# The sum over four attention heads: five VectorE products and additions, or one product and four TensorE matmuls with an identity

## The chip, the core and the metric

The kernel runs on one NeuronCore of a Trainium2 chip, in float32 throughout. The metric is the device time of one execution in microseconds, as the median of the runs made. A profiled execution, with the hardware profiler recording every instruction, is a separate execution with its own time.

## The reference, cut to what matters

The model is two graph layers over 12,500 nodes with 256 features and 200,000 edges sorted by destination. The first is a pair of GCN convolutions; the second is an attention layer with four heads of 64 channels. The change touches only the end of the second:

```python
xt = jnp.matmul(x, weight).reshape(-1, heads, out_ch)          # (n, 4, 64)
alpha_l = jnp.einsum('ehd,hd->eh', xt[row], attn_l)
alpha_r = jnp.einsum('ehd,hd->eh', xt[col], attn_r)
alpha = jax.nn.softmax(jax.nn.leaky_relu(alpha_l + alpha_r, 0.01), axis=1)
tmp = jnp.einsum('nh,nhd->nd', alpha[:n], xt[col[:n]])         # sum over 4 heads
out = jnp.broadcast_to(tmp[:, None, :], (n, heads, out_ch))
...
x = x + out
```

Only the first n = 12,500 edges matter for the output. For each of them four weights (a softmax over the heads) multiply four vectors of 64 channels of that edge's destination node; the four products are added, and the sum of 64 channels is added to each of the four quarters of the node's row.

## The kernel before, in words

`fast_path` runs in four stages. A preparation stage sorts out the chunks of edges and normalises x. Two edge stages (`convolve`, called twice) then walk over 1,563 tiles of 128 edges each: GpSimd (POOL) gathers 128 rows of a table for each tile with an indirect DMA (L1086, tile `fgot`), and TensorE (PE) multiplies them by a 0/1 matrix that adds edges to their destinations (L1091, `facc`). Each has a pool of four buffers of 14 gathered tiles, so a gather waits when PE has not yet read the buffer that it is to fill.

The last stage, the pool named `fmixes`, is the attention, and it is where the change lies. It covers 98 tiles of 128 nodes in 15 groups: 13 groups of seven tiles, one of four, one of three. Two functions do the work of a group g:

- `ends_of(g)`: for each tile of the group one matmul (`fends`, L1345, 260 columns) picks the destination rows, and ScalarE (ACT) copies the result from PSUM into the group's SBUF tile `fxg` (L1347). The `fends` PSUM tile has two buffers, so a matmul waits for the copy two before it. For groups 0 and 1 this was done earlier, in the second edge stage (tiles `fxe`). Every second group, VectorE (DVE) also makes a 0/1 matrix for later groups (`hot_t`, L1258).
- `mix(g)`: POOL gathers the group's logits (`fal`, L1355, seven indirect DMAs of 128 rows of four numbers). DVE adds the other half of the logits (L1359), for groups 0 and 1 also a correction `lacks` that PE makes with 21 small matmuls (L1326, L1361), applies the leaky ReLU, takes the maximum and subtracts it (L1362 to L1365). ACT takes the exponential (L1366). DVE sums, inverts and scales (L1367 to L1371) into the PSUM tile `share`, 4 weights for each of 128x7 nodes. Then come the lines that the change replaces: two products of two heads each, `near` into SBUF and `far` into PSUM (L1378), and three additions, `some`, `more` and `fmix` (L1381, L1383, L1385). Last, `fres` (L1387) adds the sum to the four quarters of the residual rows `fxr`, and SyncE (SP) stores the group.

The order of the work is the order of the program text, written out by hand; no scheduler moves it, and each engine runs its own instructions in order. The closing loop is

```python
for g in range(len(groups) + 2):
    if g < len(groups):
        keep(g)
        ends_of(g)
    if g >= 2:
        mix(g - 2)
```

so that every engine's list alternates: `ends_of(g)`, then `mix(g - 2)`, then `ends_of(g + 1)`, then `mix(g - 1)`. On ACT, therefore, the seven copies of group g stand before the exponential of group g - 2. On PE, before the change, the tail holds nothing but `fends` and, for the first two groups, `lacks`.

Of the kernel before, what the change touches and what calls it, by code (L numbers as in the profile page):

```python
# [8 lines left out]
F32 = mybir.dt.float32  # L9
# [8 lines left out]
P = 128  # L18
# [395 lines left out]
def fast_path(  # L414
# [26 lines left out]
    nc = tc.nc  # L441
    N, D = x.shape
    (E,) = src.shape
    H, C = attn_l.shape
# [13 lines left out]
    G = 7  # L458
# [23 lines left out]
    ident = const.tile([P, P], F32, name="fident")  # L482
# [27 lines left out]
    with tc.tile_pool(name="fprep", bufs=1) as prep:  # L510
# [86 lines left out]
        for k in range(NPT):  # L597
            p = perm[:, k, :Q[k], :]
# [23 lines left out]
        near = prep.tile([NCH, CE], F32, name="near_f")  # L622
# [51 lines left out]
        with tc.tile_pool(name="wpsum", bufs=2, space=PSUM) as psum:  # L674
# [7 lines left out]
            for i in range(KC):  # L682
                pw = psum.tile([P, D], F32, name="fw")
                for k in range(KC):
                    nc.tensor.matmul(pw, wpt[:, k, i * P:(i + 1) * P], wa[:, k, :],
                                     start=(k == 0), stop=(k == KC - 1))
                nc.scalar.activation(wf[:, i, :], pw, AF.Copy)
            pw = psum.tile([P, D], F32, name="fw")
            for k in range(KC):
                nc.tensor.matmul(pw[:1, :], bp[:, k:k + 1], wa[:, k, :], start=(k == 0),  # L690
                                 stop=(k == KC - 1))
# [158 lines left out]
        psum = wpsum.enter_context(tc.tile_pool(name="kpsum", bufs=1, space=PSUM))  # L850
# [4 lines left out]
        some = prep.tile([P, 1], F32, name="degs")  # L855
# [395 lines left out]
    def load_ends(pool, c, bufs):  # L1251
        to_all = pool.tile([P, CE], I32, name="to_all", bufs=bufs)
        nc.sync.dma_start(to_all, dst[c * CE:(c + 1) * CE].partition_broadcast(P))
        return to_all

    def turn_hots(pool, c, to_all, bufs):
        hot_t[c] = pool.tile([P, CE], F32, name="hot_t", bufs=bufs)
        nc.vector.tensor_scalar(hot_t[c], to_all, base_b[:, c:c + 1], lane,  # L1258
                                op0=ALU.subtract, op1=ALU.is_equal)
# [38 lines left out]
    with tc.tile_pool(name="fmixes", bufs=2) as mp, \  # L1298
            tc.tile_pool(name="apsum", bufs=1, space=PSUM) as psum:
        late = {c: load_ends(mp, c, 3) for c in range(EARLY, EARLY + 3)}  # L1300

        def turn_late(c):
            if c in late:
                turn_hots(mp, c, late[c], 3)
                if c + 3 < AC:
                    late[c + 3] = load_ends(mp, c + 3, 3)

        ends, kept = {}, {}


        groups = [(t, G) for t in range(0, NT - G, G)] + [(NT - G, 4), (NT - 3, 3)]
        assert G == 7 and J % G == 0

        def keep(g):
            t0, n = groups[g]
            kept[g] = mp.tile([P, G, D], F32, name="fxr", bufs=3)
            nc.sync.dma_start(kept[g][:, :n, :], kept_x[t0 * P:(t0 + n) * P, :].rearrange(
                "(c p) d -> p c d", p=P))

        def missing(g):  # L1320

            px = psum.tile([P, G, H], F32, name="lacks", bufs=1)
            for i in range(G):
                t = groups[g][0] + i
                for k in range(LW):
                    nc.tensor.matmul(px[:, i, :], hot_l[k][:, t * P:(t + 1) * P],  # L1326
                                     lates[NT - LW + k][:, DR:], start=(k == 0),
                                     stop=(k == LW - 1))
            return px

        def ends_of(g):

            t0, n = groups[g]
            if t0 < J:
                ends[g] = early[g]
                if g + 1 == J // G:
                    turn_late(1)
                return
            xa = ends[g] = mp.tile([P, G, DR], F32, name="fxg", bufs=4)
            for i in range(n):  # L1340
                c, j = divmod(t0 + i, J)
                if j == 0:
                    turn_late(c + 1)
                px = psum.tile([P, DR], F32, name="fends", bufs=2)
                nc.tensor.matmul(px, hot_t[c][:, j * P:(j + 1) * P], rows[c], start=True,  # L1345
                                 stop=True)
                nc.scalar.activation(xa[:, i, :], px, AF.Copy)  # L1347

        def mix(g):
            (t0, n), xa, xr = groups[g], ends.pop(g)[:, :groups[g][1], :], kept.pop(g)  # L1350
            xr = xr[:, :n, :]
            al = mp.tile([P, G, H], F32, name="fal", bufs=4)
            for i in range(n):
                c, j = divmod(t0 + i, J)
                nc.gpsimd.indirect_dma_start(  # L1355
                    out=al[:, i, :], out_offset=None, in_=(table_l if c else table_e)[:],
                    in_offset=bass.IndirectOffsetOnAxis(ap=src_t[:, c, j:j + 1], axis=0))
            s = mp.tile([P, G, H], F32, name="fs")[:, :n, :]
            nc.vector.tensor_add(s, al[:, :n, :], xa[:, :, D:])  # L1359
            if t0 < J:  # L1360
                nc.vector.tensor_add(s, s, missing(g))  # L1361
            nc.vector.scalar_tensor_tensor(s, s, SLOPE, s, op0=ALU.mult, op1=ALU.max)  # L1362
            m = mp.tile([P, G], F32, name="fm")[:, :n]
            nc.vector.tensor_reduce(m, s, AX.X, ALU.max)
            nc.vector.tensor_sub(s, s, m[:, :, None].to_broadcast([P, n, H]))  # L1365
            nc.scalar.activation(s, s, AF.Exp)  # L1366
            nc.vector.tensor_reduce(m, s, AX.X, ALU.add)  # L1367
            nc.vector.reciprocal(m, m)

            share = psum.tile([P, G, H], F32, name="share", bufs=1)[:, :n, :]  # L1370
            nc.vector.tensor_mul(share, s, m[:, :, None].to_broadcast([P, n, H]))  # L1371
            xh = xa[:, :, :D].rearrange("p g (h c) -> p g h c", h=H)
            h2 = H // 2
            near = mp.tile([P, h2, G, C], F32, name="near")[:, :, :n, :]
            far = psum.tile([P, h2, 512], F32, name="far", bufs=1)
            far = far[:, :, :n * C].rearrange("p h (g c) -> p h g c", c=C)
            for v, o in ((near, 0), (far, h2)):
                nc.vector.tensor_mul(v.rearrange("p h g c -> p g h c"), xh[:, :, o:o + h2, :],  # L1378
                                     share[:, :, o:o + h2, None].to_broadcast([P, n, h2, C]))
            some = mp.tile([P, G, C], F32, name="some")[:, :n, :]  # L1380
            nc.vector.tensor_add(some, near[:, 0], far[:, 0])  # L1381
            more = psum.tile([P, G, C], F32, name="more", bufs=1)[:, :n, :]
            nc.vector.tensor_add(more, near[:, 1], far[:, 1])  # L1383
            mixed = psum.tile([P, G, C], F32, name="fmix", bufs=1)[:, :n, :]
            nc.vector.tensor_add(mixed, some, more)  # L1385
            res = mp.tile([P, G, D], F32, name="fres", bufs=2)[:, :n, :]
            nc.vector.tensor_add(res.rearrange("p g (h c) -> p g h c", h=H),  # L1387
                                 xr.rearrange("p g (h c) -> p g h c", h=H),
                                 mixed[:, :, None, :].to_broadcast([P, n, H, C]))
            n0, n1 = t0 * P, min((t0 + n) * P, N)  # L1390
            k, r = divmod(n1 - n0, P)
            if k:
                nc.sync.dma_start(out[n0:n0 + k * P, :].rearrange("(c p) d -> p c d", p=P),
                                  res[:, :k, :])
            if r:
                nc.sync.dma_start(out[n0 + k * P:n1, :], res[:r, k, :])

        assert H == 4
# [6 lines that stand above are left out]
# [41 lines left out]
```

## Time and profile before

| what | value |
|---|---|
| median of 3 runs | 4234.17 us (4231.9 to 4235.17) |
| profiled execution | 4963.54 us, its span 4961.4 us |
| mean granted TensorE clock in it | 0.710 |
| busy share of the span | POOL 62%, PE 54%, DVE 24%, ACT 8% |
| attention stage in it | from the first `fends` at 4752.25 us to the end of the span, 209.2 us |
| busy in 4750 to 4962 us | DVE 108.0 us, POOL 94.1, PE 89.0, ACT 36.4 |
| `near`, `far` of a group of seven | 1.09 us each, 896 elements a partition |
| `some`, `more`, `fmix` of such a group | 0.62 to 0.63 us each, 448 elements a partition |
| `fres` of such a group | 2.02 us, 1792 elements a partition |
| `fends` | 84 matmuls in this stage, each two records of 260 columns, 587 ns mean |

A row of the table of groups reads: line, engine, operation, output<-input, shape, count, then busy microseconds and the mean nanoseconds of one, then the idle time just before and what ended it. The timeline has the start, the duration in microseconds, engine, line, operation and tiles, and in brackets the idle time before it. A float32 matmul shows as two records. Ends of PE records are modelled, not measured; the wait of the engine that needs a PE result is measured.

### The profile page before, as it was taken

The page shows a single profiled execution, that of the slowest core. Times are in us where ns is not written, and L with a number is a line of the kernel's source. Part 1 is how long each engine was busy: PE and PEld are TensorE (multiplying, and loading weights), DVE is VectorE, ACT ScalarE, POOL GpSimd, SP SyncE. Part 2 cuts the span into 40 slices and gives each one's busy share as a digit, 9 for nine tenths or more (in the row PEclk, how much of TensorE's full clock was granted, in tenths as well). Part 3 has the DMA queues.
Part 4 walks back from the last instruction along what each step waited for, and adds up shares of the span by engine and source line. Part 5 has one row for each costly group of instructions (what it writes and reads, how often), then busy time and mean ns, then how long its engine had stood idle before and what let it go on. Part 6 is the DMA issues. An engine that isn't in the chain of part 4 may idle for free. (4 is left out here: it accounts for less than half of the span.)

```text
span 4961.4 us, 31747 instructions
## 1 busy us (share of the span) xinstructions
PE 2702.2 (54%) x10363; PEld 2052.2 (41%) x10363; DVE 1215.4 (24%) x2571; ACT 408.9 (8%) x1067; POOL 3088.9 (62%) x3304
## 2 busy tenths in 40 slices
PE   5356565555555665555444555555464545555553
PEld 4244443333334444333334444444454445444441
DVE  7122111111111111111222222222122222222236
ACT  5000000000000000000000100010011001001011
POOL 1666666666666666666566666666666666666633
PEclk7667676666676676667677777777777777777766
DMA  7433333333333333333334433443343434444435
GB/s 225 115 102 105 105 107 105 105 107 104 103 103 105 106 107 104 104 105 105 111 97 113 116 105 106 110 110 107 101 111 105 111 108 109 111 114 109 108 102 158
DMA packets 325910, 551.10 MB, mean 111 GB/s; under 512 B 96009, under 2 KB 224232, under 8 KB 325736
## 3 DMA queue, kind: packets, MB, share of 16 engines
q0 software_dynamic: 153520, 414.27, 31.0%
q1 hardware_dynamic: 126678, 118.54, 7.9%
q10 hardware_dynamic: 45538, 16.17, 1.3%
q8 instruction: 86, 1.41, 0.1%
q14 instruction: 88, 0.72, 0.1%
HBM read 495.47 MB, written 53.19 MB: 111 GB/s over the span
## 5 line engine op out<-in xcount | busy, mean ns | idle before, releaser
L1086 POOL DMA_INDIRECT fgot<-ftable,fsrc_t x3126 | 2965.6, 949 | 1621.6 <-issue 911.1
L1091 PE MATMUL facc<-fgot,fhot 128*128 128x257 f32 (+1 forms) x6252 | 1876.5, 441 | 629.3 <-issue 594.5
L1091 PEld LDWEIGHTS facc<-fgot,fhot 128*128 128x128 f32 x6252 | 1350.4, 224 | 999.1 <-issue 774.1
L1037 DVE TENSOR_TENSOR buf<-buf,fturn 128x256 f32 x224 | 94.4, 422 | 2092.0 <-remote 1725.3
L1014 DVE TENSOR_TENSOR fhot<-iota_p,to_t 128x1792 f32<-128x1792 f32 x224 | 448.4, 2003 | 0.1
L1200 PE MATMUL fpt<-fident,h 128*128 128x128 f32 x194 | 59.6, 405 | 586.2 <-ACT h L1195 462.1
L1120 PE MATMUL fpo<-wf,buf 128*128 128x256 f32 x388 | 145.3, 513 | 309.7 <-DVE buf L1037 217.1
L1200 PEld LDWEIGHTS fpt<-fident,h 128*128 128x128 f32 x194 | 26.8, 187 | 625.7 <-ACT h L1195 486.3
L1120 PEld LDWEIGHTS fpo<-wf,buf 128*128 128x128 f32 x388 | 96.4, 258 | 358.5 <-issue 250.7
L1174 PE MATMUL fpo<-fwo,fz 128*128 128x256 f32 x388 | 124.8, 451 | 214.6 <-issue 122.7
L1165 DVE SCALAR_TENSOR_TENSOR fy<-rb,fb2c,fpz 128x128 f32<-128x128 f32 x194 | 58.7, 344 | 722.8 <-remote 390.5
L1021 ACT ACTIVATE fsums<-facc 128x257 f32<-128x257 f32 (+1 forms) x224 | 85.9, 383 | 1740.8 <-remote 1229.7
L1179 DVE SCALAR_TENSOR_TENSOR fx<-fpo,fdinv,fxb 128x256 f32<-128x256 f32 x97 | 46.9, 483 | 714.0 <-remote 453.9
L1174 PEld LDWEIGHTS fpo<-fwo,fz 128*128 128x128 f32 x388 | 76.8, 217 | 228.6 <-issue 125.5
L1158 PE MATMUL fpz<-buf,fwb 128*128 128x128 f32 x776 | 158.2, 372 | 12.0 <-DVE buf L1037 12.0
L977 PE MATMUL fturn<-fident,fsums 128*128 128x128 f32 x448 | 107.5, 330 | 93.8 <-ACT fsums L1021 56.8
L1213 PE MATMUL fpx<-fwg,ht 128*128 128x4 f32 (+1 forms) x388 | 62.8, 270 | 175.6 <-ACT ht L1204 119.0
L1158 PEld LDWEIGHTS fpz<-buf,fwb 128*128 128x128 f32 x776 | 150.1, 285 | 14.9 <-DVE buf L1037 13.9
L1213 PEld LDWEIGHTS fpx<-fwg,ht 128*128 128x128 f32 x388 | 64.1, 210 | 190.2 <-ACT ht L1204 125.9
L977 PEld LDWEIGHTS fturn<-fident,fsums 128*128 128x128 f32 x448 | 75.5, 175 | 146.6 <-ACT fsums L1021 67.9
L1355 POOL DMA_INDIRECT fal<-table_l,fsrc_t x84 | 80.4, 957 | 73.7 <-DVE fs L1362 49.0
L1345 PE MATMUL fends<-rows,hot_t 128*128 128x260 f32 x168 | 72.8, 587 | 92.1 <-issue 57.2
(213 smaller groups left out, 1633.8 us busy)
## 6 DMA issues: line engine op xcount, KB each, us to landing
fgot<-ftable,fsrc_t POOLq DMA_INDIRECT x3126
ftable<-fxt SPq DMA_DIRECT2D x14, 910.0 KB
self<-ftable SPq DMA_DIRECT2D x97, 130.0 KB
ftable<-fo ACTq DMA_DIRECT2D x98, 128.0 KB
kept_x<-fx SPq DMA_DIRECT2D x98, 128.0 KB
self<-ftable SPq DMA_DIRECT2D x97, 128.0 KB
fxb<-in_x_dram SPq DMA_DIRECT2D x97, 128.0 KB
fxt<-in_x_dram SPq DMA_DIRECT2D x13, 896.0 KB
```

The costliest lines, as they stand in the source:

```text
L977: nc.tensor.transpose(v["pt"][:, i * KC + k, :], rows[:, k * P:(k + 1) * P], ident)
L1014: nc.vector.tensor_tensor(h[:, :n, :], iota_p[:, None, :].to_broadcast([P, n, P]), to_t[:, c, :n, None].to_broadcast([P, n, P]), ALU.is_equal)
L1021: nc.scalar.activation(sb, acc, AF.Copy)
L1037: nc.vector.tensor_add(b, b, v["pt"][:, :KC, :])
L1086: nc.gpsimd.indirect_dma_start(out=got, out_offset=None, in_=table[:], in_offset=bass.IndirectOffsetOnAxis(ap=src_t[:, c, j:j + 1], axis=0))
L1091: nc.tensor.matmul(acc, hots[c][:, j, :], got[:, :width], start=(j == 0), stop=(j == nj[c] - 1))
L1120: nc.tensor.matmul(po, buf[:, k, :P], wf[:, k, :], start=(k == 0), stop=False)
L1158: nc.tensor.matmul(pz[:, m, :], wb[:, k, m * P:(m + 1) * P], buf[:, k, :P], start=(k == 0), stop=(k == KC - 1))
L1174: nc.tensor.matmul(po, v["z"][:, m, :], wo[:, m, :], start=(m == 0), stop=(m == KC - 1))
L1200: nc.tensor.transpose(pt[:, k, :], v["h"][:, k * P:(k + 1) * P], ident)
L1213: nc.tensor.matmul(px, v["ht"][:, k, :], wg[:, k, d0:], start=(k == 0), stop=(k == KC - 1))
L1355: nc.gpsimd.indirect_dma_start(out=al[:, i, :], out_offset=None, in_=(table_l if c else table_e)[:], in_offset=bass.IndirectOffsetOnAxis(a ...
```

## The change

The two products and three additions become one product over all four heads, written head by head into one SBUF tile `part`, and four matmuls that accumulate into one PSUM tile, each with the identity `fident` as one operand and one head's 64 channels of all the group's tiles (448 columns) as the other. `fmix` gets two PSUM buffers in place of one; the PSUM tiles `far` and `more` go.

```diff
             share = psum.tile([P, G, H], F32, name="share", bufs=1)[:, :n, :]
             nc.vector.tensor_mul(share, s, m[:, :, None].to_broadcast([P, n, H]))
-            xh = xa[:, :, :D].rearrange("p g (h c) -> p g h c", h=H)
-            h2 = H // 2
-            near = mp.tile([P, h2, G, C], F32, name="near")[:, :, :n, :]
-            far = psum.tile([P, h2, 512], F32, name="far", bufs=1)
-            far = far[:, :, :n * C].rearrange("p h (g c) -> p h g c", c=C)
-            for v, o in ((near, 0), (far, h2)):
-                nc.vector.tensor_mul(v.rearrange("p h g c -> p g h c"), xh[:, :, o:o + h2, :],
-                                     share[:, :, o:o + h2, None].to_broadcast([P, n, h2, C]))
-            some = mp.tile([P, G, C], F32, name="some")[:, :n, :]
-            nc.vector.tensor_add(some, near[:, 0], far[:, 0])
-            more = psum.tile([P, G, C], F32, name="more", bufs=1)[:, :n, :]
-            nc.vector.tensor_add(more, near[:, 1], far[:, 1])
-            mixed = psum.tile([P, G, C], F32, name="fmix", bufs=1)[:, :n, :]
-            nc.vector.tensor_add(mixed, some, more)
+
+            part = mp.tile([P, H, G, C], F32, name="part")[:, :, :n, :]
+            nc.vector.tensor_mul(part.rearrange("p h g c -> p g h c"),
+                                 xa[:, :, :D].rearrange("p g (h c) -> p g h c", h=H),
+                                 share[:, :, :, None].to_broadcast([P, n, H, C]))
+            mixed = psum.tile([P, G, C], F32, name="fmix", bufs=2)[:, :n, :]
+            for h in range(H):
+                nc.tensor.matmul(mixed, ident, part[:, h], start=(h == 0), stop=(h == H - 1))
             res = mp.tile([P, G, D], F32, name="fres", bufs=2)[:, :n, :]
```

On PE the four matmuls of `mix(g - 2)` now stand after the `fends` (and `lacks`) of its iteration and before the `fends` of group g + 1; on DVE `fres` follows the product directly.

## The prediction

> **What bounds the kernel now.** I read the page first, for where the time lies, then POOL's waits, then the timeline and windows of the attention stage, which alone the change touches. The gathers of the two edge stages fill most of the span:
>
> ```profile
> L1086 POOL DMA_INDIRECT fgot<-ftable,fsrc_t x3126 | 2965.6, 949 | 1621.6 <-issue 911.1
> ```
>
> A gather is 949 ns and the step to the next some 0.29 us. Of the 1621.6 us that POOL idles before gathers, 911.1 is that step; most of the rest is in these two rows of its waits:
>
> ```profile
> POOL fgot L1086 <- remote: 465.1, 116, 11.4
> POOL fgot L1086 <- PE facc L1091: 158.7, 18, 10.8
> ```
>
> With three small rows behind PE (20.6, 5.3 and 4.2) that is 654 us in which POOL waits for a buffer that PE should long have read. The profiled execution took 4963.5 us, of which 2.1 lies around the span, the runs 4234.2: 729 less. The two numbers are nearly the same once the attention stage is added, where PE shows the same sickness:
>
> ```profile
> 4857.51 0.39 ACT L1347 ACTIVATE fxg<-fends 128x260 f32<-128x260 f32 x1 [5.22 <-remote]
> 4857.95 1.24 PE L1345 MATMUL fends<-rows,hot_t 128*128 128x260 f32 x2 [4.38 <-ACT fxg L1347]
> ...
> 4862.40 0.39 ACT L1347 ACTIVATE fxg<-fends 128x260 f32<-128x260 f32 x1 [4.50 <-remote]
> ```
>
> ACT's copy needs nothing but the matmul, yet waits 4.5 to 5.2 us for one that is modelled at 1.24. There are three such spells: DVE waits 18.7 us for `lacks` until 4785.90, the next five `fends` take some 20 us instead of 5, DVE's sum after the exponential waits 14.9 us at 4869.96 and 10.95 at 4914.01. That is 18.7 + 15 + 14.9 + 11 = 60 us; 654 + 60 = 714 of the 729. I conclude that the spells belong to the profiled execution and that the timed attention stage is about 209 - 70 = 140 us. So I read its pace between the spells:
>
> ```profile
> 4837.47 0.18 DVE L1359 TENSOR_TENSOR fs<-fal,fxg 128x28 f32<-128x28 f32 x1
> ...
> 4838.40 0.23 ACT L1366 ACTIVATE fs<-fs 128x28 f32<-128x28 f32 x1 [2.12 <-issue]
> ...
> 4838.96 5.33 PE L1345 MATMUL fends<-rows,hot_t 128*128 128x260 f32 x14 [1.73 <-issue]
> 4839.12 0.20 DVE L1371 TENSOR_TENSOR share<-fs,fm 128x28 f32<-128x28 f32 x1
> 4839.35 1.09 DVE L1378 TENSOR_TENSOR near<-fxg,share 128x896 f32<-128x896 f32 x1
> 4840.35 1.09 DVE L1378 TENSOR_TENSOR far<-fxg,share 128x896 f32<-128x896 f32 x1
> 4841.47 0.62 DVE L1381 TENSOR_TENSOR some<-near,far 128x448 f32<-128x448 f32 x1
> 4842.01 0.62 DVE L1383 TENSOR_TENSOR more<-near,far 128x448 f32<-128x448 f32 x1
> 4842.67 0.63 DVE L1385 TENSOR_TENSOR fmix<-some,more 128x448 f32<-128x448 f32 x1
> 4843.33 2.02 DVE L1387 TENSOR_TENSOR fres<-fxr,fmix 128x1792 f32<-128x1792 f32 x1
> 4845.27 1.21 DVE L1258 TENSOR_SCALAR hot_t<-to_all,base_b,lane 128x1792 f32<-128x1792 int32 x1
> 4846.39 0.18 DVE L1359 TENSOR_TENSOR fs<-fal,fxg 128x28 f32<-128x28 f32 x1
> ```
>
> DVE is never idle here but for the exponential: a group is 8.92 us with `hot_t` (4837.47 to 4846.39), 7.80 without, 8.36 on average. PE's seven `fends` for the group three ahead lie wholly beside `near` to `fres`. DVE bounds this stage and PE has room, but only in parallel.
>
> **The change part by part.** *Removed:* `near` to `fmix`, 4839.35 to 4843.33, 3.98 us of DVE a group.
>
> *Added on DVE:* one product of 1792 elements. `fres` has as many, 2.02 us, and two starts of 896 (1.00 apart) give the same. Saving on DVE alone: 1.96.
>
> *Added on PE:* four float32 matmuls of 448 columns. At half clock seven `fends` follow each other every 0.87 us (ACT's copies at 4842.28 and 4843.15), 3.35 ns a column; the shortest and longest `fends` records, 382 and 802 ns, say that full clock halves it. So 448 columns are 1.50 us at half and 0.75 at full clock, four of them 6.0 or 3.0, and 0.3 for fill and the last result: 6.3 or 3.3. The eight loads of the identity (0.28 us each in the mean of the `fends` loads) run beside the matmul before them: nothing; with no cover they would add 2. DVE has nothing between `part` and `fres`, so it stands still for all of it.
>
> *Moved:* the order of `fends`. On PE the four matmuls stand ahead of the next seven `fends`, and they wait for `part`, which waits for the exponential, which on ACT stands behind the previous seven copies. What lay side by side is now one ring: exponential to `share` 0.95 (4838.40 to 4839.35), `part` 2.02, hand-over 0.05, the four matmuls 3.3, seven `fends` 4.2 (x14 in 4.25 us at 4879.17, at full clock paced by the copies), last copy 0.45: 10.97 us a group at full clock. At half clock it is 0.95 + 2.02 + 0.05 + 6.3 + 6.1 + 0.45 = 15.87. DVE's `fres`, `hot_t` and logits (1.94 + 1.12 + 0.93 = 4.0 at most) hide beside the `fends`; without that cover they would add up to 4. POOL's seven `fal` (8.75 us at 1.25) and SP's loads and stores keep their places and have more time than now: nothing. The second `fmix` buffer: nothing, since DVE waits for each result anyway.
>
> *The clock.* Each ring has one PE pause: copy, exponential, product, 3.5 us. The row:
>
> ```profile
> 4884.50:4887.80 3.30, 0.83 (x4) 0.68 (x4) 2.74 (x9) 0.87 (x4) 2.68 (x3) 1.00 0.46 148
> 4888.00:4891.20 3.20, 3.20 (x8) 2.16 (x8) 3.13 (x5) 1.31 (x5) 2.45 (x3) 0.50 1.01 296
> 4891.40:4894.60 3.20, 0.90 (x4) 0.30 (x2) 3.19 (x3) 0.14 (x1) 2.59 (x3) 1.00 0.40 114
> ```
>
> (stretch, length, busy PE, PE load, DVE, ACT, POOL, then the clock.) PE was busy for 0.83 of 3.30 us, and for the next stretch the clock was 0.50, then 1.00 again after a full one. The Trainium skill ("TensorE: Matmul & The Clock Gate", Part 1: The HAM clock gate) has the clock halved after an idle window of about 3.4 us. By its rule, a pause of 3.5 us almost never covers a whole free-running window, the ring stays at 10.97, and the sum below becomes +33. By the row, a window that is a quarter busy already costs the next one. I take the row: one window of 3.4 us at half clock in each ring loses 1.7 us, 12.6 us a group.
>
> *The sum.* Groups 1 to 11: 11 x (12.6 - 8.36) = 46.6. Group 0: `part` and the cold matmuls, 8.4, fall in front of the `fends` and `lacks` that follow, which set the pace there. The last two `fends` groups have four and three matmuls instead of seven: 7 x 0.6 = -4.2. Group 12 has no `fends` behind it: 2.02 + 0.05 + 3.3 or 6.3 - 3.98 = 1.4 or 4.4; the groups of four and three tiles likewise 0.7 or 2.4 and 0.5 or 1.8 (256 and 192 columns, 1.22 and 0.95 for the product by their `fres`, less 2.59 and 2.12); PE is cold there, so 8.6. Together +59 us, on a stage of 140. Ends: +33 at full clock; at half clock throughout 11 x 7.5 + 8.4 - 6.1 + 8.6 = +93. Nothing outside the stage moves, so these stand on the median: 4234 + 59 = 4293.
>
> **The rivals.** *Full clock.* The long dense bursts (3 us of matmuls, then 4 of `fends`) keep it up: for it, 4874 to 4888 us holds 1.00 over a pause of 3.07. Against it, the row above. 4267.
>
> *Half clock.* The pause recurs in every ring and the second half of the burst, paced by copies, counts as thinly busy; the stage's clock was 0.50 in many stretches. 4327.
>
> *Spells in the timed runs.* If PE falls there too into the pace of 4.9 us for 260 columns, 448 columns cost 34 us for four matmuls; three groups so hit add some 85 to the forecast, 4380. The 714 of 729 speak against it.
>
> *Faster.* If, against that account, the 60 us of spells in the attention stage are in the timed runs, and PE's denser work keeps it out of them, the time falls by 60 and rises by 33: 4207. It decides when more than 33 us of spells vanish at full clock. That DVE's 1.96 x 15 = 29 us is simply gained is excluded: `fres` reads the four matmuls' result and is next on DVE.
>
> **How the numbers follow.** The ring with one cold window a group 0.52 (its own range 4275 to 4312), full clock 0.21, half clock 0.17, spells 0.05, faster 0.04, and 0.01 for a loss that all but vanishes. The range, 4258 to 4335, runs from just under full clock to just over half clock and leaves out the last three cases, 0.10, and the outer edges of the first three. A change under 0.2% (8.5 us) is about what measurement can't tell from none: faster 0.04, same 0.01, slower 0.95.
>
> **What the profile would show.** Right: `part` near 2.0 us x13; DVE idle 3.3 to 6.3 us before `fres`, released by PE `fmix`; the `fends` of a group starting only after `fmix`, no longer beside DVE's products; starts of L1359 some 12 to 13 us apart between spells; POOL's edge stages unchanged. Wrong: `fres` following `part` within 2 us, or `fends` before `fmix` of the same ring; records of `fmix` at half the length reckoned (then 448 columns are cheaper than 3.35 ns each); a stage that was never bound by DVE in the timed runs, so that 8.36 is not the pace before.

## The result, and the profile after

The changed kernel takes 4301.09 us (4300.27 to 4304.73) against 4233.03 (4230.73 to 4235.17): 68 us more, a ratio of 1.0162 with a 95% interval of 1.0150 to 1.0174. The forecast was 4293 with a range of 4258 to 4335. The runs below come from three chips: on the first, which has these two times' pace, the kernel before takes 4234 us, on the other two 4967 and 4956, so every ratio is to the kernel before on the same chip. Where the runs of one kernel scatter, its ratio leaves out those more than 1.5% above the fastest, so that it can differ a little from the quotient of the two medians.

The rows of the page after that answer to the gathers' row of before, and the new row of the four matmuls (columns as in the table of groups):

```profile
L1086 POOL DMA_INDIRECT fgot<-ftable,fsrc_t x3126 | 2972.7, 951 | 985.3 <-issue 899.8
...
L1379 PE MATMUL fmix<-part,fident 128*128 128x448 f32 (+2 forms) x120 | 83.8, 876 | 59.2 <-DVE part L1374 59.2
```

The gathers are as they were, 951 ns each and 899.8 us of steps between them, but the 636 us of other waiting has gone from their row. This profile has none of the spells in which PE fell behind; its execution took 4301.55 us, within the timed runs. So it must not be set against the first profile of before, and the first experiment takes another. The loss lies where the change is, in the waits of the attention stage (us in total, times, longest):

```profile
DVE fres L1381 <- PE fmix L1379: 86.3, 15, 6.4
...
PE fmix L1379 <- DVE part L1374: 59.2, 15, 7.1
POOL fal L1355 <- DVE fs L1362: 38.6, 7, 9.0
```

DVE and PE now stand still for each other, 15 times each. POOL's wait for a logits buffer is new too; it costs nothing, since the logits are there in time. One ring in the timeline (start, duration, engine, line, tiles, idle time before):

```profile
4176.51 0.22 ACT L1366 ACTIVATE fs<-fs 128x28 f32<-128x28 f32 x1
...
4177.44 2.02 DVE L1374 TENSOR_TENSOR part<-fxg,share 128x1792 f32<-128x1792 f32 x1
...
4179.60 6.22 PE L1379 MATMUL fmix<-part,fident 128*128 128x448 f32 x8 [3.42 <-DVE part L1374]
...
4185.66 4.15 PE L1345 MATMUL fends<-rows,hot_t 128*128 128x260 f32 x14
...
4185.86 2.02 DVE L1381 TENSOR_TENSOR fres<-fxr,fmix 128x1792 f32<-128x1792 f32 x1 [6.41 <-PE fmix L1379]
...
4188.93 0.18 DVE L1359 TENSOR_TENSOR fs<-fal,fxg 128x28 f32<-128x28 f32 x1
...
4190.13 0.22 ACT L1366 ACTIVATE fs<-fs 128x28 f32<-128x28 f32 x1
```

From exponential to exponential 13.62 us: 0.93 to `part`, 2.16 to the first matmul, 6.06 to the first `fends`, 4.19 to ACT's last copy (4189.85), 0.28 to the exponential. `fends` no longer lie beside DVE's products. The same ring cut into windows (stretch, length, busy PE, PE load, DVE, ACT, POOL, then the clock, the DMA share and GB/s):

```profile
4178.80:4182.20 3.40, 2.60 (x4) 1.40 (x5) 0.66 (x1) 0.00 (x0) 2.48 (x4) 0.50 0.65 216
4182.20:4185.60 3.40, 3.40 (x5) 1.46 (x5) 0.00 (x0) 0.00 (x0) 0.86 (x1) 0.50 0.04 1
4185.60:4189.00 3.40, 3.32 (x13) 1.76 (x11) 3.14 (x3) 1.88 (x5) 0.00 (x0) 1.00 0.04 15
4189.00:4192.40 3.40, 0.77 (x3) 0.30 (x2) 2.58 (x9) 0.94 (x4) 2.42 (x3) 1.00 1.02 316
```

All four matmuls run at half clock, all `fends` at full clock. The stretches lie, to 0.03 us, on the grid of 3.41 us on which the granted clock changes (here at 4178.77, 4185.60 and 4192.43). After the window in which PE is busy for 0.77 us the clock is halved for the next two; a window with 2.60 us does not raise it again; the full one does, just as the matmuls end. The starts of the exponentials from group 2 on lie 13.43, 13.54, 13.60, 13.62, 13.64, 13.65, 13.65 and 13.65 us apart: the ring runs into four windows of 3.41 us and stays there.

### The profile page after: what moved, and what is told of

It reads as the page before. It is cut to its first block, busy times and chain, and to the rows that moved or that the text cites. A ratio compares the mean times of both kernels' runs of the same rounds, so it can differ in the third digit from the quotient of the medians.

```text
span 4299.8 us, 31939 instructions
## 1 busy us (share of the span) xinstructions
PE 3194.5 (74%) x10483; PEld 1967.3 (46%) x10483; DVE 1191.5 (28%) x2511; ACT 412.3 (10%) x1067; POOL 3095.8 (72%) x3304
## 5 line engine op out<-in xcount | busy, mean ns | idle before, releaser
L1086 POOL DMA_INDIRECT fgot<-ftable,fsrc_t x3126 | 2972.7, 951 | 985.3 <-issue 899.8
L1091 PE MATMUL facc<-fgot,fhot 128*128 128x257 f32 (+1 forms) x6252 | 2400.9, 501 | 939.5 <-DMA fgot<-ftable,fsrc_t 897.2
L1091 PEld LDWEIGHTS facc<-fgot,fhot 128*128 128x128 f32 x6252 | 1256.6, 233 | 1927.4 <-DMA fgot<-ftable,fsrc_t 1496.2
L1379 PE MATMUL fmix<-part,fident 128*128 128x448 f32 (+2 forms) x120 | 83.8, 876 | 59.2 <-DVE part L1374 59.2
L1125 ACT ACTIVATE fo<-fpo,fdinv 128x256 f32<-128x256 f32 x97 | 45.9, 473 | 787.4 <-PE fpo L1121 787.4
L1158 PE MATMUL fpz<-buf,fwb 128*128 128x128 f32 x776 | 120.6, 307 | 0.0
L1158 PEld LDWEIGHTS fpz<-buf,fwb 128*128 128x128 f32 x776 | 117.8, 229 | 2.0 <-DVE fy L1165 0.2
L977 PE MATMUL fturn<-fident,self 128*128 128x128 f32 x396 | 85.3, 301 | 27.3 <-DMA self<-ftable 23.3
L1053 DVE COPY buf<-buf 128x640 f32<-128x640 f32 x194 | 102.6, 529 | 3.3
L1121 PE MATMUL fpo<-bb,fins 2*128 2x256 f32 x194 | 84.6, 522 | 0.0
L1204 ACT ACTIVATE ht<-fpt 128x256 f32<-128x256 f32 x97 | 37.2, 383 | 474.2 <-PE fpt L1200 474.2
```

The costliest lines, as they stand in the source:

```text
L977: nc.tensor.transpose(v["pt"][:, i * KC + k, :], rows[:, k * P:(k + 1) * P], ident)
L1053: nc.vector.tensor_copy(nxt[:, :, :BW - P], buf[:, :, P:])
L1086: nc.gpsimd.indirect_dma_start(out=got, out_offset=None, in_=table[:], in_offset=bass.IndirectOffsetOnAxis(ap=src_t[:, c, j:j + 1], axis=0))
L1091: nc.tensor.matmul(acc, hots[c][:, j, :], got[:, :width], start=(j == 0), stop=(j == nj[c] - 1))
L1121: nc.tensor.matmul(po, fs, bb, start=False, stop=True)
L1158: nc.tensor.matmul(pz[:, m, :], wb[:, k, m * P:(m + 1) * P], buf[:, k, :P], start=(k == 0), stop=(k == KC - 1))
```

## The experiments

**The kernel before, once more, on the first chip** (no edit), since its only profile had the spells.

> The kernel before, once more, for a second profile. Theory (the spells of slow TensorE belong to that one profiled execution): time near 4233 us again; if this profile has no spells, its span is near the timed runs and its attention stage, from the first fends to the end, is about 140 us with L1359 starting 7.8 or 8.9 us apart. Rival (the spells are in every execution): the span is far above the runs again or the stage is again about 209 us in a span near the runs.

It took 4235.35 us. POOL's waits, and two groups of its attention stage in the timeline:

```profile
POOL fgot L1086 <- issue: 904.7, 2970, 0.3
...
POOL fgot L1086 <- PE facc L1091: 28.9, 95, 0.3
```

```profile
4124.93 0.18 DVE L1359 TENSOR_TENSOR fs<-fal,fxg 128x28 f32<-128x28 f32 x1
...
4126.41 6.24 PE L1345 MATMUL fends<-rows,hot_t 128*128 128x260 f32 x14 [4.04 <-ACT fxg L1347]
...
4132.72 0.18 DVE L1359 TENSOR_TENSOR fs<-fal,fxg 128x28 f32<-128x28 f32 x1
...
4134.21 5.33 PE L1345 MATMUL fends<-rows,hot_t 128*128 128x260 f32 x14 [1.56 <-ACT fs L1366]
```

POOL waits for PE for 28.9 us here and not for 654, and no single wait is over 0.3. The groups are 7.79 us (4124.93 to 4132.72) and 8.93 (to 4141.65) apart, the pace that was read between the spells. The attention stage, from the first `fends` at 4087.89 to the end at 4233.3, is 145.4 us; after the change it is 4086.14 to 4299.8, 213.7. The difference, 68.3, is the whole loss. By the starts of the exponentials it splits as follows:

| part of the stage | before, us | after, us | difference |
|---|---|---|---|
| first `fends` to the exponential of group 2 | 37.97 | 49.80 | 11.8 |
| from there to the one of group 10, eight steps | 67.31 | 108.78 | 41.5 |
| from there to the one of group 14 | 29.17 | 41.96 | 12.8 |
| from there to the end | 10.96 | 13.12 | 2.2 |

**The matmuls one ring later.** The four matmuls and `fres` of a group are given out one iteration later, so that neither PE nor DVE waits for the other in the same ring. The load of the residual rows (`keep`) moves to the end of the iteration. Only the loop is shown, with notes; the functions that it calls hold the lines of the changed kernel.

```diff
-        for g in range(len(groups) + 2):
+        for g in range(len(groups) + 3):
             if g < len(groups):
-                keep(g)
                 ends_of(g)
-            if g >= 2:
+            if g >= 3:
+                add_heads(g - 3)      # the four matmuls
+            if 2 <= g < len(groups) + 2:
                 mix(g - 2)            # ends with the product, part
+            if g >= 3:
+                finish(g - 3)         # fres and the store
+            if g < len(groups):
+                keep(g)
```

> The changed kernel with the four matmuls of a group issued one iteration later, after the next group's fends, and fres after the next group's product; nothing else differs but that the fxr load is issued at the iteration's end. Theory (the order on TensorE makes a ring of exponential, product, matmuls and fends, and its pause halves the clock): TensorE always has ready work, so a group costs the most of TensorE 7.3, VectorE 6.5 and GpSimd 8.75 us: 4225 to 4240 us, all of the 68 us gone. Rival 1 (TensorE's work itself is too long): 4.1 plus 3 us a group is nothing to save, 4290 us or more. Rival 2 (TensorE stays at half clock whatever the order): 12.4 us a group, about 4280 us.

4233.24 us, ratio 0.9996 [0.9987, 1.0005]: all 68 us are gone, with the same product and the same matmuls. PE in the timeline:

```profile
4128.45 3.17 PE L1356 MATMUL fmix<-part,fident 128*128 128x448 f32 x8
4131.46 4.15 PE L1345 MATMUL fends<-rows,hot_t 128*128 128x260 f32 x14
4135.45 3.17 PE L1356 MATMUL fmix<-part,fident 128*128 128x448 f32 x8
4138.45 4.15 PE L1345 MATMUL fends<-rows,hot_t 128*128 128x260 f32 x14
```

PE runs without a pause, the matmuls take 3.17 us, and a group takes 7.00 us while it lasts. Why the kernel is then no faster than before can be read from the stage as one window (before first, then this kernel) and in DVE's waits of this kernel:

```profile
4088.00:4233.00 145.00, 75.20 (x252) 48.41 (x252) 108.39 (x202) 34.73 (x100) 95.77 (x98) 0.71 0.68 211
```

```profile
4087.00:4232.00 145.00, 108.25 (x372) 65.69 (x371) 81.56 (x142) 36.01 (x100) 95.30 (x98) 0.84 0.67 211
```

```profile
DVE fs L1367 <- DMA fal<-table_l,fsrc_t: 23.5, 8, 6.6
...
DVE fs L1367 <- DMA fal<-table_e,fsrc_t: 9.5, 2, 6.1
```

DVE is busy for 81.56 us in place of 108.39, and waits for the gathered logits for 33. POOL's 98 gathers of 0.95 us with 0.30 between them are 122 of the stage's 145 us. So POOL's gathers seem to come next once DVE is relieved; the last experiment tries that and doesn't settle it.

**The pause filled.** Four matmuls with operands that are long there, into a PSUM tile that nobody reads, stand on PE between the `fends` and the four real ones, so that the ring keeps its order but PE's pause shrinks to 0.32 us.

```diff
+            idle = psum.tile([P, G * C], F32, name="idle", bufs=1)
+            for i in range(4):
+                nc.tensor.matmul(idle, ident, hot_l[0][:, :G * C], start=True, stop=True)
             nc.vector.scalar_tensor_tensor(s, s, SLOPE, s, op0=ALU.mult, op1=ALU.max)
```

> The changed kernel with four matmuls of 448 columns on constant data, into a PSUM tile that nobody reads, put on TensorE between a group's fends and its fmix, where it now pauses 3.4 us. Theory (the pause halves the clock for all of fmix): the pause is filled for 3.0 us, fmix takes 3.1 to 3.3 us instead of 6.2, a group 10.5 instead of 13.65: about 4263 us (4255 to 4275). Rival (the clock has no share in the loss): fmix as long as before and the time no less than 4301; if the added matmuls are not hidden by the pause, up to 4340 us.

4266.16 us, ratio 1.0077 [1.0060, 1.0094]. PE in the timeline, and three windows:

```profile
4152.57 3.27 PE L1382 MATMUL fmix<-part,fident 128*128 128x448 f32 x8 [0.32 <-DVE part L1377]
4155.69 4.15 PE L1345 MATMUL fends<-rows,hot_t 128*128 128x260 f32 x14
4159.67 3.17 PE L1364 MATMUL idle<-hot_l,fident 128*128 128x448 f32 x8
4163.16 3.27 PE L1382 MATMUL fmix<-part,fident 128*128 128x448 f32 x8 [0.32 <-DVE part L1377]
```

```profile
4152.50:4155.90 3.40, 3.32 (x9) 1.82 (x10) 0.03 (x2) 0.00 (x0) 2.67 (x3) 1.00 0.52 149
4155.90:4159.30 3.40, 3.29 (x13) 1.74 (x12) 2.66 (x5) 2.11 (x6) 2.49 (x4) 1.00 0.18 48
4159.30:4162.70 3.40, 3.40 (x10) 1.65 (x10) 2.19 (x4) 0.72 (x3) 2.49 (x4) 1.00 1.00 300
```

With more work on PE the kernel is 35 us faster than the changed one. In these rings the clock stays at 1.00 and a ring is 10.59 us. What remains above before, 32 us, is about the price of the order alone; the other 35 are the clock's. The forecast's full-clock case had a ring of 10.97 and 33 us.

**One matmul in place of four.** Heads 1 to 3 are left out of the sum.

```diff
-            for h in range(H):
-                nc.tensor.matmul(mixed, ident, part[:, h], start=(h == 0), stop=(h == H - 1))
+            nc.tensor.matmul(mixed, ident, part[:, 0], start=True, stop=True)
```

> The changed kernel with one matmul instead of four; heads 1 to 3 are left out of the sum. Theory (ring): exponential, product, one matmul of 0.8 to 1.6 us and the seven fends still follow one another, 9 to 11.2 us a group: 4241 to 4265 us, slower than before although VectorE has less to do and TensorE next to nothing more. Rival (only the length of the four matmuls counts, not their place): VectorE's 7.5 us a group, less than before's 8.36: about 4223 us.

4246.75 us, ratio 1.0028 [1.0018, 1.0038]. PE in the timeline:

```profile
4182.39 0.99 PE L1378 MATMUL fmix<-part,fident 128*128 128x448 f32 x2 [3.42 <-DVE part L1374]
4183.21 5.22 PE L1345 MATMUL fends<-rows,hot_t 128*128 128x260 f32 x14
4191.86 1.83 PE L1378 MATMUL fmix<-part,fident 128*128 128x448 f32 x2 [3.42 <-DVE part L1374]
```

and, from another ring of it,

```profile
4154.55 0.99 PE L1378 MATMUL fmix<-part,fident 128*128 128x448 f32 x2 [3.42 <-DVE part L1374]
4155.37 4.15 PE L1345 MATMUL fends<-rows,hot_t 128*128 128x260 f32 x14
```

DVE has less work than before and PE 1 to 2 us of new work in a group, but the exponentials of groups 2 to 10 lie 9.7 us apart (4131.61 to 4209.51, eight steps) against 8.4 before. The pause of 3.42 us is there, and the `fends` run partly at half clock, 5.22 us. In the second cut the clock doesn't fall, and that ring takes 8.39 us (exponentials at 4151.45 and 4159.84), no more than a group before. So, by that ring, what this kernel loses from group to group it loses through the clock: the ring makes the pause, and the pause makes work slow that is cheap in itself.

**The pause made longer.** One addition of 448 columns on DVE, unread, between `share` and `part`.

```diff
+            extra = mp.tile([P, G, C], F32, name="extra", bufs=1)[:, :n, :]
+            nc.vector.tensor_add(extra, xa[:, :, :C], xa[:, :, C:2 * C])
             part = mp.tile([P, H, G, C], F32, name="part")[:, :, :n, :]
```

> The changed kernel with one more VectorE addition of 448 elements (0.62 us) between share and part, its result unread. Theory (the ring is locked to four windows of the clock of 3.41 us, fmix ending where the clock rises, so that a later start of fmix is made up by the end of it at full clock): ring still 13.65 us, 4300 to 4303 us. Rival (the ring is just the sum of its steps): 13.65 plus 0.6 a group, 4309 to 4311 us.

On the second chip, 5005.61 us, ratio 1.0067 [1.0047, 1.0087]. The total says little, since the changed kernel was not run on that chip; the rings do. PE in the timeline:

```profile
4888.02 5.85 PE L1381 MATMUL fmix<-part,fident 128*128 128x448 f32 x8 [3.82 <-DVE part L1376]
4893.71 4.15 PE L1345 MATMUL fends<-rows,hot_t 128*128 128x260 f32 x14
4901.68 5.85 PE L1381 MATMUL fmix<-part,fident 128*128 128x448 f32 x8 [3.83 <-DVE part L1376]
```

The pause is 0.40 us longer and the matmuls are 0.39 us shorter: the ring stays at 13.66.

**The pause made shorter.** The sum and reciprocal of the softmax are left out, so that the weights aren't normalised (they are multiplied by the maximum, which still lies in `m`) and DVE comes to `part` sooner.

```diff
             nc.scalar.activation(s, s, AF.Exp)
-            nc.vector.tensor_reduce(m, s, AX.X, ALU.add)
-            nc.vector.reciprocal(m, m)
```

> The changed kernel without the sum and the reciprocal of the softmax (two VectorE steps, 0.45 us, left out between exponential and share, so the weights are not normalised). Theory (locked ring): fmix then starts at the edge of a clock window, the first window counts as busy and the clock rises one window earlier in part of the rings; a group falls by more than the 0.45 us taken away, to 11.9 to 13.2 us: 4282 to 4296 us. Rival (the sum of the steps): 15 times 0.45, 4294 to 4295 us. Rival 2 (locked, with no cliff): 4300 to 4302 us.

4979.03 us, ratio 1.0009 [0.9989, 1.0029]. PE in the timeline:

```profile
4855.17 3.25 PE L1376 MATMUL fmix<-part,fident 128*128 128x448 f32 x8 [2.97 <-DVE part L1371]
...
4865.37 3.25 PE L1376 MATMUL fmix<-part,fident 128*128 128x448 f32 x8 [2.97 <-DVE part L1371]
```

A pause shorter by 0.45 us (3.42 to 2.97) gives rings of 10.20 us in this stretch, 3.45 less than 13.65. Two windows on the clock's edges show why:

```profile
4860.07:4863.48 3.41, 2.25 (x8) 0.89 (x6) 2.66 (x8) 2.05 (x6) 1.21 (x2) 1.00 0.63 208
4863.48:4866.90 3.42, 1.53 (x4) 0.87 (x5) 1.74 (x1) 0.00 (x0) 2.56 (x3) 1.00 1.03 326
```

The pause (4862.40 to 4865.37) now lies across an edge, and each of the two windows that share it still has 1.53 us of PE work or more. The clock does not fall: it is 1.00 from 4846.42 to 4897.61, where the expectation had it rise one window earlier. So 10.20 us is the sum of the steps at full clock, by the filled pause 10.59 - 0.45 = 10.14. It doesn't hold for the whole stage: a pause of 3.67 us leaves the window from 4894.20 with only 0.95 us of work, and the next has half clock again. The exponentials of groups 3 to 6 are 10.20 us apart, the later ones up to group 10 10.9 to 13.15. From group 2 to 10 a ring is 11.26 us on average, 2.3 less than in the changed kernel for 0.45 us of work removed.

**Changed and delayed kernel again, together,** on the third chip, to set their totals side by side.

> The changed kernel again, beside the others of this set. Where the kernel before takes 4234 us: 4301. Where it takes 4967 us: the edge stages wait for TensorE as before, and in the attention stage the ring of 13.65 us stands against groups that lose some 60 us in spells: 4967 + 68 - 30 = about 5005 us, by the delayed kernel's 5005.6 there.

> The changed kernel with one more VectorE addition (0.62 us) between share and part, beside the changed kernel itself. Theory (ring locked to four clock windows): the same time as the changed kernel within 2 us. Rival (sum of the steps): 8 us more (13 times 0.62).

The changed kernel took 4987.34 us, ratio 1.0044 [1.0017, 1.0071], the delayed one 4993.28, ratio 1.0094 [1.0066, 1.0121]. Their medians are 6 us apart, and the runs of each scatter over 60 us and more; the totals can't tell the theory's 0 from the rival's 8 us. The rings do again. The exponentials of the changed kernel run from 13.03 over 13.36, 13.51 and 13.59 to 13.65 us apart as on the first chip, and the delayed kernel's matmuls start 13.65 apart (4902.25 to 4915.90). On this chip the change was expected to cost 38 us, 68 less 30 us of spells; the interval of its ratio is 8 to 35 us. Why it costs less than on the first is outside what the experiments explain.

**The later ring with earlier gathers.** To see what the relieved DVE is worth: the 14 gathers of groups 0 and 1 moved ahead of the attention stage, with the one-ring-later order, and the same move alone in the kernel before. The tile of the last rows was narrowed to make room in SBUF; the cut below leaves that out, and the later order too.

```diff
+        als = {}
+        for g in range(J // G):
+            als[g] = ap.tile([P, G, H], F32, name="fal_e", bufs=J // G)
+            for i in range(G):
+                j = g * G + i
+                nc.gpsimd.indirect_dma_start(
+                    out=als[g][:, i, :], out_offset=None, in_=table_e[:],
+                    in_offset=bass.IndirectOffsetOnAxis(ap=src_t[:, 0, j:j + 1], axis=0))
...
-            al = mp.tile([P, G, H], F32, name="fal", bufs=4)
-            for i in range(n):
+            al = als[g] if t0 < J else mp.tile([P, G, H], F32, name="fal", bufs=4)
+            for i in range(n if t0 >= J else 0):
```

> The order of e1_next_ring, and besides the 14 logit gathers of groups 0 and 1 issued on GpSimd straight after the last gather of rows, 8 us earlier than now, into tiles of their own. Theory (with the matmuls out of the ring the stage is bound by GpSimd's 98 gathers of 1.25 us): about 8 us less than e1_next_ring: 4223 to 4228 us. Rival (something else bounds e1_next_ring): 4231 to 4235 us.

> The kernel before with the same earlier gathers and nothing else. Theory (VectorE's 8.36 us a group bounds it, GpSimd's 8.75 only just): the first mix starts up to 6 us earlier, 4227 to 4231 us, less gain than e5_ring_early by 1 to 6 us. Rival (both kernels are bound by the gathers alone): the same time as e5_ring_early.

> The order of e1_next_ring with the 14 gathers of groups 0 and 1 issued 8 us earlier. Where the kernel before takes 4234 us, theory: 4223 to 4228 us (bound by GpSimd's gathers, which start earlier); rival: 4231 to 4235. Where it takes 4967: about 4960 us.

> The kernel before with the same earlier gathers. Where the kernel before takes 4234 us, theory: 4227 to 4231 us, 1 to 6 us above f3_ring_early_again since VectorE's 8.36 us a group takes over; rival: the same time as f3_ring_early_again. Where it takes 4967: about the same as before.

| kernel | second chip | third chip |
|---|---|---|
| later ring, earlier gathers | 4962.85 us, 0.9986 [0.9970, 1.0003] | 4938.06 us, 0.9964 [0.9944, 0.9984] |
| before, earlier gathers | 4967.63 us, 0.9993 [0.9974, 1.0013] | 4956.63 us, 1.0008 [0.9978, 1.0038] |

On the third chip the pair of edits beats both kernels, by 18 us against before; on the second the gain is not told from none, and the earlier gathers alone give nothing on either. The forecast was about 8 us, so the cause given for it, POOL's gathers, isn't shown by the 18. The later ring alone was not run on these two chips, nor the pair of edits on the first: how much of the gain belongs to which edit, and what it is worth on the first chip, is open.

## Why the prediction was right

The direction and the mechanism held, and so did most of the parts; one term was too small.

*Right, the durations.* The product took 2.02 us, the four matmuls 6.22 to 6.25 at half clock and 3.17 to 3.27 at full clock (forecast 2.02, 6.3, 3.3), the `fends` at full clock 4.15 (4.2). DVE's wait before `fres` was 5.1 to 6.4 us in the groups of seven, inside the 3.3 to 6.3 but for a tenth.

*Right, the ring.* That the order makes a ring, and that the ring with its pause is the loss and not the matmuls' own length, is shown by the later ring, which has every instruction of the change and none of its loss, and from the other side by one matmul in place of four, which still loses 12.6 us.

*Right, the row and not the rule.* The row of before, a quarter-busy window that costs the next one, held: after 0.77 of 3.40 us the clock falls. (At 1.53 of 3.42 us, in the shorter pause, it did not.) The Trainium skill ("TensorE: Matmul & The Clock Gate", Part 1: The HAM clock gate) has the clock fall after an idle window; with idle read as no work at all, as the prediction read it, the clock would have stayed up and the sum would have been +33. The filled pause shows that world: +32. The same section's free-running window of about 3.4 us is what the rings show, and its way back, a busy window of that length, fits the 2.60 us that did not suffice.

*Mis-sized, the cold window.* The step that was too small is "one window of 3.4 us at half clock in each ring loses 1.7 us, 12.6 us a group". It took the first window after the pause to raise the clock whatever lay in it. But that window begins inside the pause, so it is only 76% busy and raises nothing; a second cold one follows, and the matmuls run at half clock to their end. The clock's part is 13.65 - 10.59 = 3.06 us a ring by the filled pause, in place of 1.7. A smaller error the other way hid part of it: the ring at full clock was put at 10.97 in place of 10.59, 4 us in eleven rings, so that +33 comes so near to the +32 measured is in part luck. (And 10.97 + 1.7 is 12.7, not 12.6.) In the eight steps from group 2 to 10 the forecast gives 8 x 4.24 = 33.9 us and the trace 41.5: 7.6 of the 9 us by which the total was short. The head of the stage was put at 8.4 + 4.2 = 12.6 and measured 11.8; what comes after group 10 was put at 12.9 and measured 15.0.

*Wrong, where the spells are from.* "I conclude that the spells belong to the profiled execution" is not so. On the second and third chip every timed run of the kernel before, 48 and 67 of them, took 4917 to 5001 us, and the profiles taken there, of the other kernels, have the spells. So has that of the kernel before with earlier gathers (second chip):

```profile
POOL fgot L1086 <- remote: 528.5, 132, 11.5
```

On the first chip a profile has none and takes no longer than the timed runs. The pace goes with the chip, or with a condition that it was in: each chip was measured at one time only, so chip and hour can't be told apart, and on which chip the first profile of before was taken is not recorded. The arithmetic, 714 of 729 us, was right (the stage is 145.4 us where it gave about 140). That the forecast held is luck in this one respect: the changed kernel was timed at the fast pace. What causes the spells stays open. So does how much of the change's loss they hide: the ratio on the third chip is lower than on the first.

## What to carry to other kernels

Work moved from a busy engine to one with room gains only if no engine's ordered list makes the two wait for each other within one iteration; give the second engine's part out one iteration later, and look at once for the resource that comes next (here probably POOL's gathers): the later ring took the loss away and gained nothing. When a loop leaves PE a pause of about a clock window, ask how much PE works in the windows that hold the pause, not only how long the pause is: 0.40 us more was worth nothing here, 0.45 us less was worth up to 3.4 us a ring. And before a single profile is used to read a stage, set its span against the timed runs; where they differ, ask which chip each came from.

## What the runs showed of the hardware that was not expected

A loop through PE can lock to the clock's windows. With pauses of 3.42 and 3.82 us the ring was 13.65 us both times, four windows of 3.41. In the changed kernel its distance to 13.65 about halved with each ring (0.48, 0.22, 0.11, 0.05, 0.03, 0.01 us), and on the third chip, from another start, likewise (0.62, 0.29, 0.14, 0.06). Work done before the edge at which the clock rises takes twice as long as work after it, which would give that halving; this is worked out and was not tried by itself. The rings of 10.20 us with a pause of 2.97 us are no such lock: they had no half-clock window, and three windows would be 10.24.

PE's busy share in the records, whose ends are modelled, is not all that the clock goes by. In the changed kernel the window from 4113.93 to 4117.34 was busy for 3.37 us, from 4115.02 on with `lacks` matmuls of 4 columns, and the clock was 0.50 in the next.

The same kernel at 4234 us on one chip and at 4956 to 4967 on two others was the largest difference of the whole study, ten times that of the change.
